# Sharing the centre tap of a row-transformed convolution between even and odd pixels, and squaring two groups of keys in one instruction

## The chip, the cores and the metric

The kernel runs on one core of a Trainium2 chip. The metric is the device time of one execution in microseconds; the time before is the median of three runs. The core has five engines that run beside each other: TensorE (PE in the profile) multiplies matrices and writes to PSUM, VectorE (DVE) and ScalarE (ACT) work element by element and read PSUM or SBUF, GpSimd (POOL) works on SBUF alone, and SyncE (SP) issues nearly all transfers. Everything is fp32.

## The reference

The input has 4 images of 128 channels and 128 x 128 pixels. Layer 0 normalises groups of 4 channels, then treats each pixel as a token of 128 channels:

```
t = LN0(x);  t = t + (silu(LN1(t)) @ W_out.T)
wht = LN2(t) @ W_whiten.T
k = square(relu(wht @ W_key.T))            # 512 hidden keys
t = t + sigmoid(wht @ W_recep.T) * (k @ W_value.T)
```

It does that for the image and for its transpose. No step mixes pixels, so both give the same, and x = x + 2t. Layer 1 normalises groups again and computes

```
x + (conv3x3(gn(x), weight[0], padding 1) + bias) * sigmoid(relu(avg @ w1.T) @ w2.T)
```

The weights of the convolution are always expert 0's, 128 to 128 channels.

## The kernel before, in words

**Layer 0** works on groups of 1024 pixels (`layer0(g)`, g from 0 to 63, 16 for each image), each of two halves of 512 (h = 0, 1). A half's tokens are normalised three times (`norm`, statistics by `bn_stats` on DVE at L770, roots by POOL at L820), go through attention (`att`, L954) and are turned back to channels by way of a DRAM buffer. Then the half has four blocks of 128 keys (j = 0 to 3): a matmul `pk` (L1033) into PSUM, `re` on ACT (L1038: relu and bias, PSUM to an SBUF tile `h`), a square, and a matmul `kv` (L1071) that adds the block's values in one PSUM bank. The squares are on ACT in place (`sq`, L1044), or on DVE as (key + bias) times the rectified key (`sqd`, L1050). `SQUARES` gives the engine for each block: DDAA for both halves while g is under 17, AAAA after.

**Layer 1** works on blocks of 16 rows (`conv(k)`, k from 0 to 31, 8 for each image). The block has four sets of four rows, and a transform along the rows makes six products from six shifted rows: DVE forms v0 to v5 from the rows by sums and differences (L1179 to L1193, twelve instructions of 512 elements, both inputs in SBUF), TensorE convolves each along the row with its own three transformed taps (`product(i)`, three matmuls at L1203 to L1205), and the results m0 to m5 are combined to four output rows: ACT moves m1 and m3 to SBUF (`e`, L1218 and L1226), DVE does the rest (`ab`, `cd`, `y`, L1222 to L1239). The columns shifted by one pixel leave out the edge, hence 512, 508 and 508 columns. `conv_setup(b)` scales the taps (`us`, L621) and adds the identity to four centre taps (`ut2`, L627), once for each image.

**The order.** Each instruction is entered in a planner (`op`, class `Plan`) with its engine, an estimated cost, a priority (its group number plus `SHIFT` by name), what it reads and writes, and the buffers it opens. The planner plays the whole program through once with these costs and fixes the order on each engine; each engine then runs its instructions in that order. `LOOK` and `HASTE` weigh priority against readiness, `ROOM` gives the number of buffers of each kind (PSUM: `Bh` 3 for keys, `Bkv` 1, `Btr` 2 for attention and transposes, `Bconv` 2 for products), and `port` marks instructions that the planner keeps apart on DVE and POOL. The convolution of image b has priorities that lie among the groups of image b + 1, so it runs beside layer 0 of the next image; the last image's convolution has nothing beside it.

**The start.** All of image 0 is loaded in eight pieces and its statistics are taken on DVE; their aggregate (L493) goes to PE as small matmuls (L498, L500) for the group means. `FIRST_FILL` puts warm-up matmuls (`hot`, L411) on PE when the pieces 6 and 7 arrive, three and two of them; more are put into planned gaps of PE early on (`busy`).

Of the kernel before, what the change touches and what calls it, by code (L numbers as in the profile page):

```python
# [23 lines left out]
    "R": -94.694, "Rc": 15.085, "Rm": -2.646, "S": 24.009, "T": -84.8, "Tz": -36.19, "W": -22.14,  # L24
    "ab": 37.315, "att": 1.644, "b": 31.731, "bn0": 11.794, "bn1": -17.35, "bn2": -15.592,
    "bx": 49.609, "c": 7.82, "cag": 6.719, "cav": -18.068, "cd": -103.804, "cp": -37.768,
    "cp1": -27.368, "cpm": -17.233, "cpr": -71.755, "cpv": -65.194, "cre": 48.407, "crt": -73.005,
    "csg": -26.086, "csp": -39.311, "cth": -29.247, "cve": 53.942, "e": 12.136, "e0": 14.7,
    "e1": -70.81, "e2": -55.971, "edge": 60.492, "fw": 14.887, "g": -16.106, "gag": -13.379,
    "gnb": -14.148, "gpm": -2.701, "gpv": -23.531, "grt": -1.635, "gsp": -6.989, "gve": -30.013,  # L30
    "hot": -13.329, "in": 26.361, "in0": 105.375, "kv": 3.816, "late": 12.753, "m0": 23.5,
    "m1": -101.213, "o": -54.585, "pk": 3.497, "pq": -18.954, "pr": 3.288, "q": -106.007,
    "raw": -61.508, "rc": -6.337, "re": -93.796, "silu": -97.676, "sq": -115.033, "sqd": -34.912,
    "t": -2.49, "tD": -49.255, "tR": 16.588, "tW": -20.948, "th": -60.823, "tt": 105.266,
    "u": 16.271, "us": -19.465, "ut": 67.807, "ut2": 9.337, "uw": -50.513, "v": 57.985, "w": 117.982,
    "w0": 44.736, "w1": -43.048, "w2": -6.943, "x": 70.181, "x1": -70.076, "xc": 6.78, "xd": 2.407,
    "xf": -58.371, "xo": -10.863, "xs": -54.606, "y": 24.867, "z": 15.121, "zD": 21.243,
    "zR": 18.813, "zW": -13.966,
}
SQUARES = (("DDAA", "DDAA"), ("AAAA", "AAAA"))  # L40
TAIL_BANKS = ("Bkv", "Btr", "Btr", "Bh", "Bconv", "Bh")
TAIL_HOMES = ("xc", "xc", "x", "x", "x", "xc", "xc", "x")
CONV_AT, CONV_STEP = 2.0, 2.0
LOOK = {'PE': 0.018, 'DVE': 0.087, 'ACT': 0.048, 'POOL': 0.004, 'SP': 0.048}
HASTE = 31.975
SQUARES_AT = 17
ROOM = dict(
    x=3, xd=2, xs=2, ut=3, t=7, z=2, y=2, zd=2, zc=2, td=2, tt=2, R=2, y2=2, h=6, r=2, xc=2, vt=3, v=4,
# [3 lines left out]
BACKLOG = 1.96  # L52
FIRST_U_ON_DVE = (2, 3)


XF_BUS, FIRST_XD, LATE_AT = 3.4, -25, -5
FILL_UNTIL, FILL_STEP = 330, 1.2
FIRST_FILL = {6: 3, 7: 2}
# [26 lines left out]
def S_ON(g):  # L85
    return "POOL" if T_BY_DMA(g) else "DVE"

# [155 lines left out]
def conv_preact_kernel(  # L243
# [42 lines left out]
        z=[P, SUB, C], y=[P, CH], y2=[P, CH], h=[P, CH], r=[P, CH],  # L286
        xc=[P, BLK_ROWS + 2, W], vt=[P, Q, W], v=[P, Q, W], yt=[P, Q, W], uw=[P, 3, P],
# [17 lines left out]
    def staged(name, n, src=None):  # L305
        t = sb.tile([P, n], F32, tag="h", name=name, bufs=ROOM["h"])
        if src is not None:
            nc.scalar.dma_start(t, src)
        return t
# [112 lines left out]
    READ, WRITE = (0, 0.85), (0, 0.4)  # L422

    def op(name, eng, cost, prio, emit, reads=(), writes=(), new=(), port=False, bus=0.0):
        return plan.op(name, eng, cost, prio + SHIFT.get(name, 0.0), emit, reads, writes, new, port, bus)
# [112 lines left out]
    def conv_setup(b, at):  # L538
# [90 lines left out]
        for i in (1, 2, 3, 4, 0, 5):  # L629
            t = ("uw", b, i)  # L630
            if b > 0:

                def fetch(i=i, t=t):
                    nc.sync.dma_start(make(t, "uw"), raw_u[i])

                op("uw", D, READ, at - 1, fetch, [(("raw", i), 0), (("ready", b - 1), 0)], [(t, 0)], [(t, "uw")], bus=0.65)
            op(
                "us", V, (0.52, 0.61), at, lambda i=i: scaled(i), [(c, 0), (t, 0)],
                [(t, 0), *([(("ready", b), 0)] if i == 5 else ())], (), True,
            )  # L640
            if i in TAP:
                op("ut2", V, (0.21, 0.29), at, lambda i=i: tapped(i), [(t, 0)], [(t, 0)], (), True)

# [92 lines left out]
    def layer0(g):  # L736
# [3 lines left out]
        if p * PAIR % PER == 0:  # L740
# [6 lines left out]
            for q in range(SUB):  # L747

                on_dve = k == 0 and q in FIRST_U_ON_DVE

                def lay(q=q, on_dve=on_dve):
                    rs, nb = gn0[b]
                    scale, bias = rs[:, q : q + 1], nb[:, q : q + 1]
                    if on_dve:
                        nc.vector.tensor_scalar(T[xd][:, q], T[xd][:, q], scale, bias, ALU.mult, ALU.add)
                    else:
                        nc.scalar.activation(T[xd][:, q], T[xd][:, q], AF.Identity, bias=bias, scale=scale)

                op(
                    "u", V if on_dve else A, (0.61, 0.7) if on_dve else (0.705, 0.82), g, lay, [(("gn0", b), 0), *((xd, a) for a in range(SUB))],  # L760
                    [(xd, ("u", q))],
                )
# [117 lines left out]
        for h in range(PAIR):  # L880
            r = (p * PAIR + h) % PER

            def turn(h=h, r=r):
# [5 lines left out]
                "ut", V, (0.61, 0.7), g, turn, [(xd, ("u", q)) for q in range(SUB)],  # L889
# [105 lines left out]
        for h in range(PAIR):  # L995
# [33 lines left out]
            for j in range(NH):  # L1029
                pk, hh = ("pk", g, h, j), ("h", g, h, j)  # L1030
# [6 lines left out]
                def relu(pk=pk, hh=hh, j=j):  # L1037
                    nc.scalar.activation(make(hh, "h"), T[pk], AF.Relu, bias=kbias[:, j : j + 1])  # L1038

                op("re", A, (0.572, 0.69), g, relu, [(pk, 0)], [(hh, 0)], [(hh, "h")])  # L1040
                if square_on(g, h, j) == "A":

                    def square(hh=hh):
                        nc.scalar.activation(T[hh], T[hh], AF.Square)  # L1044

                    op("sq", A, (0.52, 0.63), g, square, [(hh, 0)], [(hh, 0)])
                else:

                    def square(pk=pk, hh=hh, j=j):
                        nc.vector.scalar_tensor_tensor(  # L1050
                            T[hh], T[pk], kbias[:, j : j + 1], T[hh], ALU.add, ALU.mult
                        )

                    op("sqd", V, (0.605, 0.685), g, square, [(hh, 0), (pk, 0)], [(hh, 0)])
# [11 lines left out]
            for j in range(NH):  # L1066

                def value(j=j, kv=kv, h=h):
                    if j == 0:
                        make(kv, "Bkv")  # L1070
                    nc.tensor.matmul(T[kv], wv[:, j, :], T["h", g, h, j], start=(j == 0), stop=(j == NH - 1))  # L1071
# [3 lines left out]
                    [(("wv", "c"), 0), (("h", g, h, j), 0), *([(kv, j - 1)] if j else ())],  # L1075
# [32 lines left out]
    def conv(k, at):  # L1108
# [29 lines left out]

        def units(s):
# [8 lines left out]
        def put(n, tag):  # L1148
            if tag == "v" and ending:
                t = sb.tile([P, CH], F32, tag="h", name=n, bufs=ROOM["h"])  # L1150
                T[name_of(n)] = t.rearrange("p (q w) -> p q w", w=W)
                return T[name_of(n)]
            return make(name_of(n), tag)

        def do(name, eng, cost, fn, reads=(), writes=(), new=(), port=False):
            new = [(t, "h" if tag == "v" and ending else tag) for t, tag in new]
# [3 lines left out]
        TWO = (0.605, 0.685)  # L1160

        def inner(name, tag, fn, rows_in=(), tiles_in=(), extra=(), cost=TWO, inplace=False):
# [7 lines left out]
            else:  # L1170
                reads += [(("turned", k - 1, half), v) for v in HALVES[half]]
            do(
                "v" if tag == "v" else "pq", V, cost, fn, reads + ([(t, 0)] if inplace else []), writes,
                () if inplace else [(t, tag)], True,
# [3 lines left out]

        inner("p", "vt", lambda: stt(put("p", "vt"), rows(2), -4.0, rows(4), ALU.mult, ALU.add), (2, 4))  # L1179
        inner("q", "vt", lambda: stt(put("q", "vt"), rows(1), -4.0, rows(3), ALU.mult, ALU.add), (1, 3))  # L1180
        inner(
            "v1", "v", lambda: stt(put("v1", "v"), get("p"), gn["mg6"], get("q"), ALU.add, ALU.add), (),  # L1182
            ("p", "q"), [(("gn1", b), 0)], (0.655, 0.73),
        )
        inner("v2", "v", lambda: tt(put("v2", "v"), get("p"), get("q"), ALU.subtract), (), ("p", "q"))
        inner("p2", "vt", lambda: tt(put("p2", "vt"), rows(4), rows(2), ALU.subtract), (2, 4))
        inner("q2", "vt", lambda: tt(put("q2", "vt"), rows(3), rows(1), ALU.subtract), (1, 3))
        inner("v3", "v", lambda: stt(put("v3", "v"), get("q2"), 2.0, get("p2"), ALU.mult, ALU.add), (), ("p2", "q2"))
        inner("v4", "v", lambda: stt(put("v4", "v"), get("q2"), -2.0, get("p2"), ALU.mult, ALU.add), (), ("p2", "q2"))
        inner("v0a", "v", lambda: tt(put("v0", "v"), rows(0), rows(2), ALU.subtract), (0, 2))  # L1190
        inner("v0b", "v", lambda: stt(get("v0"), get("v0"), 4.0, get("p2"), ALU.mult, ALU.add), (), ("p2",), inplace=True)
        inner("v5a", "v", lambda: tt(put("v5", "v"), rows(5), rows(3), ALU.subtract), (5, 3))
        inner("v5b", "v", lambda: stt(get("v5"), get("q2"), -4.0, get("v5"), ALU.mult, ALU.add), (), ("q2",), inplace=True)  # L1193

        def product(i):
            tag = TAIL_BANKS[i] if ending else "Bconv"
            m, v = name_of(f"m{i}"), name_of(f"v{i}")

# [9 lines left out]

        def t0(n):
            return (name_of(n), 0)  # L1210

        def outer(name, fn, reads, writes, new=(), port=False):
# [5 lines left out]
            lambda: nc.scalar.activation(put("e1", "yt"), get("m1"), AF.Identity, bias=gn["beta"]),  # L1218
            [t0("m1"), (("gn1", b), 0)], [t0("e1")], [(name_of("e1"), "yt")],
        )  # L1220
        product(2)
# [4 lines left out]
            "e", A, (0.572, 0.69), lambda: nc.scalar.copy(put("e3", "yt"), get("m3")), [t0("m3")],  # L1226
            [t0("e3")], [(name_of("e3"), "yt")],
        )
        product(4)
# [91 lines left out]
```

## Time and profile before

| | us |
|---|---|
| median of 3 runs | 1742.97 (1740.23 to 1747.48) |
| profiled execution | 1742.63 |
| its span, first to last instruction | 1740.9 |
| busy: PE, DVE, ACT, POOL | 1690.7, 1424.9, 1293.8, 1184.0 |
| granted TensorE clock | 0.997 |

Busy time is that in which at least one instruction of the engine was in flight. In the groups, a row gives the line of the kernel, the engine, the operation, output and inputs with shapes and the count, then the busy time, the mean time of one in ns, and the idle time of the engine before them with what ended it. An fp32 matmul shows as two records, and instructions in sequence overlap a little: for what one costs in a row, the timeline's starts are compared.

### The profile page before, as it was taken

The numbers are of one execution on the slowest core, as the hardware profiler recorded it, in microseconds if no ns is written. First come the engines' busy times: TensorE is split into PE (matmuls) and PEld (weight loads), VectorE is DVE, ScalarE is ACT, GpSimd is POOL, SyncE is SP. The second block draws the span as 40 slices with busy tenths as digits, with TensorE's granted clock in tenths as the row PEclk, the third lists the DMA queues.
The fourth block names the chain that finished last, engine by engine and source line by source line (L and its number), as shares of the span: only waits on it lengthen the run. The fifth ranks groups of instructions, "written<-read, shape, count | busy, mean of one in ns | idle before, by whom it ended". The sixth has DMA issues, their size and how long they took to land.

```text
span 1740.9 us, 18709 instructions
## 1 busy us (share of the span) xinstructions
PE 1690.7 (97%) x4872; PEld 815.7 (47%) x4872; DVE 1424.9 (82%) x2619; ACT 1293.8 (74%) x2656; POOL 1184.0 (68%) x1085
## 2 busy tenths in 40 slices
PE   5899999999999999999999999999999999999999
PEld 2444544444444445444445445454544444444443
DVE  5898888788889967798998887888897766448986
ACT  1999998898988887889889877998887875440000
POOL 1778887788987885879777886988878773310000
PEclk9999999999999999999999999999999999999999
DMA  9366675466577777578778877577776565215321
GB/s 326 91 213 202 193 219 194 145 206 230 153 250 246 252 230 236 199 232 247 250 245 245 254 238 240 178 218 236 241 254 199 183 204 176 101 75 224 154 98 73
DMA packets 140170, 354.66 MB, mean 204 GB/s; under 512 B 19079, under 2 KB 78750, under 8 KB 122782
## 3 DMA queue, kind: packets, MB, share of 16 engines
q1 hardware_dynamic: 139472, 352.99, 63.1%
q8 instruction: 39, 0.64, 0.2%
q14 instruction: 69, 0.57, 0.1%
q10 hardware_dynamic: 590, 0.46, 0.1%
HBM read 230.31 MB, written 123.07 MB: 203 GB/s over the span
## 4 chain that ended last, share of the span: by engine, by line
PE 71%; ACT 10%; POOL 8%; DVE 7%; DMA 2%; issue 2%; SPq 0%; ACTq 0%; DVEq 0%; POOLq 0%
PE kv L1071 19%; PE pk L1033 18%; PE m L1203 7%; PE m L1204 7%; PE m L1205 7%; PE att L954 5%; PE pr L1058 5%; ACT t L839 2%; ACT h L1038 2%; POOL rs L820 2%; ACT z L839 2%; DVE st L770 1%; ACT h L1044 1%; POOL x L1026 1%; POOL t L908 1%
## 5 line engine op out<-in xcount | busy, mean ns | idle before, releaser
L1071 PE MATMUL kv<-h,wv 128*128 128x512 f32 x1024 | 525.8, 598 | 4.6 <-DVE r L1080 2.6
L1033 PE MATMUL pk<-y,wk_s 128*128 128x512 f32 x1024 | 480.9, 595 | 4.7 <-ACT h L1038 3.1
L1038 ACT ACTIVATE h<-pk,kbias 128x512 f32<-128x512 f32 x512 | 336.1, 682 | 90.9 <-PE pk L1033 88.3
L1033 PEld LDWEIGHTS pk<-y,wk_s 128*128 128x128 f32 x1024 | 190.0, 190 | 239.3 <-issue 178.1
L1071 PEld LDWEIGHTS kv<-h,wv 128*128 128x128 f32 x1024 | 183.0, 190 | 205.3 <-issue 164.1
L1044 ACT ACTIVATE h<-h 128x512 f32<-128x512 f32 x444 | 267.5, 629 | 2.6
L1086 POOL TENSOR_TENSOR x<-x,r 128x512 f32<-128x512 f32 x128 | 169.8, 1327 | 132.0 <-DVE r L1080 128.5
L820 POOL TENSOR_TENSOR rs<-rs,nhalf 128x8 f32<-128x8 f32 (+1 forms) x134 | 227.2, 1700 | 47.3 <-ACT rs L817 45.1
L839 ACT ACTIVATE z<-t,nb,rs 128x128 f32<-128x128 f32 x512 | 208.7, 489 | 21.8 <-POOL nb L825 20.9
L839 ACT ACTIVATE t<-ut,nb,rs 128x128 f32<-128x128 f32 x512 | 209.7, 488 | 8.5 <-POOL nb L825 4.8
L908 POOL TENSOR_TENSOR t<-t,g 128x512 f32<-128x512 f32 x124 | 161.2, 1301 | 68.0 <-ACT t L839 67.6
L770 DVE BATCH_NORM_STATS2 st<-t 128x6 f32<-128x256 f32 x512 | 187.1, 410 | 22.9 <-POOL t L911 22.7
L1203 PE MATMUL m<-v,uw 128*128 128x512 f32 x384 | 197.7, 596 | 3.9 <-DVE v L1182 3.9
L1204 PE MATMUL m<-v,uw 128*128 128x508 f32 x384 | 195.4, 590 | 0.0
L1205 PE MATMUL m<-v,uw 128*128 128x508 f32 x384 | 194.9, 589 | 0.0
L1015 POOL TENSOR_TENSOR y<-tt,R 128x512 f32<-128x512 f32 x96 | 130.9, 1367 | 59.8 <-PE pk L1033 46.9
L1026 POOL TENSOR_TENSOR x<-tt,x 128x512 f32<-128x512 f32 x124 | 162.5, 1324 | 3.9 <-DMA tt<-ts 3.7
L911 POOL TENSOR_TENSOR t<-t,b 128x512 f32<-128x512 f32 x124 | 162.7, 1319 | 2.6
L954 PEld LDWEIGHTS att<-wo,y 128*128 128x128 f32 x1024 | 130.9, 192 | 51.7 <-issue 33.1
L1063 ACT ACTIVATE r<-pr,rbias 128x512 f32<-128x512 f32 x128 | 87.1, 681 | 72.6 <-PE pr L1058 36.2
L1058 PE MATMUL pr<-y,wr_s 128*128 128x512 f32 x256 | 132.3, 600 | 3.9 <-ACT h L1038 3.0
L954 PE MATMUL att<-wo,y 128*128 128x128 f32 x1024 | 132.8, 276 | 0.4 <-ACT y L947 0.3
(160 smaller groups left out, 2278.6 us busy)
## 6 DMA issues: line engine op xcount, KB each, us to landing
xd<-in_x SPq DMA_DIRECT2D x128, 256.0 KB
x<-in_x SPq DMA_DIRECT2D x32, 1024.0 KB
xo<-x SPq DMA_DIRECT2D x32, 1024.0 KB
R<-rd SPq DMA_DIRECT2D x63, 512.0 KB
ts<-td SPq DMA_DIRECT2D x248, 128.0 KB
tt<-ts SPq DMA_DIRECT2D x62, 512.0 KB
out<-xc SPq DMA_DIRECT2D x31, 1024.0 KB
xc<-xo SPq DMA_DIRECT2D x24, 1152.0 KB
```

The lines of the kernel that those rows point to most:

```text
L770: nc.vector.bn_stats(st[:, i : i + 2, :].rearrange("p n f -> p (n f)"), two)
L820: nc.gpsimd.tensor_tensor(T[rs][:, part], T[rs][:, part], nhalf[:, :k], ALU.pow)
L839: nc.scalar.activation(dst[:, s, :], src[:, s, :], AF.Identity, bias=nb[:, i : i + 1], scale=rs[:, i : i + 1])
L954: nc.tensor.matmul(pa[:, ts(m, P)], T[y][:, ts(m, P)], wo2, start=True, stop=True)
L1033: nc.tensor.matmul(make(pk, "Bh"), wk_s[:, ts(j, P)], T[y2], start=True, stop=True)
L1038: nc.scalar.activation(make(hh, "h"), T[pk], AF.Relu, bias=kbias[:, j : j + 1])
L1044: nc.scalar.activation(T[hh], T[hh], AF.Square)
L1058: nc.tensor.matmul(make(pr, "Bh"), wr_s, T[y2], start=True, stop=True)
L1071: nc.tensor.matmul(T[kv], wv[:, j, :], T["h", g, h, j], start=(j == 0), stop=(j == NH - 1))
L1203: nc.tensor.matmul(pc, u[:, 1], vv, start=True, stop=False)
L1204: nc.tensor.matmul(pc[:, :, 1:W], u[:, 0], vv[:, :, 0 : W - 1], start=False, stop=False)
L1205: nc.tensor.matmul(pc[:, :, 0 : W - 1], u[:, 2], vv[:, :, 1:W], start=False, stop=True)
```

## The change

Write x[2k] and x[2k+1] for even and odd pixels, and u0, u1, u2 for a product's three taps. Then

```
y[2k]   = u1 (x[2k] + x[2k+1]) + (u2 - u1) x[2k+1] + u0 x[2k-1]
y[2k+1] = u1 (x[2k] + x[2k+1]) + (u0 - u1) x[2k]   + u2 x[2k+2]
```

The first term is shared. In the products 0, 1, 3 and 5 of images 0 to 2 (`PARITY`), v is stored as an even half and an odd half (elements 256 positions apart), DVE adds the halves (`su`, 256 elements), PE computes the shared term once in the first half of a `Btr` bank (`cm`) and the four other terms in half-size matmuls (`c`), and DVE adds the shared term to both pixels after the result has been moved or summed (`cs`, reading PSUM). The differences of taps are made once for each image and product (`ud`). Products 2 and 4, and all of image 3, stay as they were.

The tile `h` now holds two blocks of keys, three tiles in place of six. A `W` in `SQUARES` squares both blocks in one ACT instruction of 1024 elements; for g under 17 three squares of a group are on DVE in place of four, one is a single on ACT and four are two wide ones.

The rest: one buffer in place of two for `zd` and `td`, the last image's v and some set-up tiles in another buffer, new values in `SHIFT`, `LOOK` and `HASTE`, three warm-up matmuls fewer. What `FIRST_U` adds leaves the engines of the first block's four instructions as they were; `RUSH`, `SUMS_ON_POOL` and the squares on POOL (`P`) are empty.

```diff
-SQUARES = (("DDAA", "DDAA"), ("AAAA", "AAAA"))
+SQUARES = (("DAWW", "DDWW"), ("WWWW", "WWWW"))
+SUM_BANK = "Btr"
-LOOK = {'PE': 0.018, 'DVE': 0.087, 'ACT': 0.048, 'POOL': 0.004, 'SP': 0.048}
-HASTE = 31.975
+LOOK = {'PE': 0, 'DVE': 0, 'ACT': 0.177, 'POOL': 0, 'SP': 0.026}
+HASTE = 75.103
 ROOM = dict(
-    x=3, xd=2, xs=2, ut=3, t=7, z=2, y=2, zd=2, zc=2, td=2, tt=2, R=2, y2=2, h=6, r=2, xc=2, vt=3, v=4,
+    s=2, ud=4,
+    x=3, xd=2, xs=2, ut=3, t=7, z=2, y=2, zd=1, zc=2, td=1, tt=2, R=2, y2=2, h=3, r=2, xc=2, vt=3, v=4,
...
-XF_BUS, FIRST_XD, LATE_AT = 3.4, -25, -5
+XF_BUS, FIRST_XD, LATE_AT = 3.2, -25, -5
-FIRST_FILL = {6: 3, 7: 2}
+FIRST_FILL = {7: 2}
...
+def PARITY(k):
+    return (0, 1, 3, 5) if k < 24 else ()
...
+                    nc.vector.tensor_tensor(make(ud, "ud"), u[:, 0::2], u[:, 1:2].to_broadcast([P, 2, P]), ALU.subtract)
+                op("ud", V, (0.335, 0.42), at, beside, [(t, 0)], [(ud, 0)], [(ud, "ud")], True)
...
+                elif how == "W" and not first:
                     def square(hh=hh):
-                        nc.scalar.activation(T[hh], T[hh], AF.Square)
+                        x = T[hh].rearrange("p a b -> p (a b)")
+                        nc.scalar.activation(x, x, AF.Square)
+                    op("sq", A, WIDE, g, square, [(hh, 0), (hh, 1)], [(hh, 0), (hh, 1)])
...
+            if tag == "v" and int(n[1]) in halves:
+                whole = T[name_of(n)].rearrange("p q w -> p (q w)")
+                T[name_of(n)] = whole.rearrange("p (e q k) -> p q k e", e=2, q=Q)
...
+                    nc.vector.tensor_tensor(dst, x[:, 0], x[:, 1], ALU.add)
+                do("su", V, (0.335, 0.42), both, [(v, 0)], [(su, 0)], [(su, "s")], True)
...
+                    bank = make(m, tag)
+                    pc = bank.rearrange("p (e q k) -> p e q k", e=2, q=Q)
+                    T[m] = bank.rearrange("p (e q k) -> p q k e", e=2, q=Q)
+                    u, d, x = T["uw", b, i], T[ud], flat_halves(i)
+                    nc.tensor.matmul(pc[:, 0], d[:, 1], x[:, 1], start=True, stop=False)
+                    nc.tensor.matmul(pc[:, 0, :, 1:], u[:, 0], x[:, 1, :, : W // 2 - 1], start=False, stop=True)
+                    nc.tensor.matmul(pc[:, 1], d[:, 0], x[:, 0], start=True, stop=False)
+                    nc.tensor.matmul(pc[:, 1, :, : W // 2 - 1], u[:, 2], x[:, 0, :, 1:], start=False, stop=True)
+
+                def shared():
+                    nc.tensor.matmul(make(mm, SUM_BANK)[:, : CH // 2], T["uw", b, i][:, 1], T[su], start=True, stop=True)
...
+            def add():
+                t = by_parity(get(n))
+                row = T[name_of(f"mm{i}")][:, : CH // 2].rearrange("p (q k o) -> p q k o", q=Q, o=1)
+                tt(t, row.to_broadcast([P, Q, W // 2, 2]), t, ALU.add)
+            do("cs", V, TWO, add, [(name_of(f"mm{i}"), 0), t0(n)], [t0(n)])
...
         product(0)
-        outer("y", lambda: tt(rows(1), get("m0"), get("c"), ALU.add), [t0("m0"), t0("c")], units(1))
+        with_shared(0, "c")
+        outer("y", lambda: tt(par(0, rows(1)), get("m0"), par(0, get("c")), ALU.add), [t0("m0"), t0("c")], units(1))
```

## The prediction

> **What bounds the kernel now.** I read the page first: TensorE is busy in nine tenths or more of nearly every slice.
>
> ```profile
> PE 1690.7 (97%) x4872; PEld 815.7 (47%) x4872; DVE 1424.9 (82%) x2619; ACT 1293.8 (74%) x2656; POOL 1184.0 (68%) x1085
> ...
> PE   5899999999999999999999999999999999999999
> ...
> DVE  5898888788889967798998887888897766448986
> ```
>
> The average hides three stages, so I cut the span where the first convolution products begin (about 425) and where the last image's convolution is left alone (about 1575). The view by stretches gives busy microseconds for each engine:
>
> ```profile
> 0.00:425.00 425.00, 386.19 (x1273) 197.55 (x1274) 351.15 (x689) 359.93 (x766) 316.98 (x329) 0.99 0.65 203
> 425.00:1575.00 1150.00, 1146.34 (x3228) 548.18 (x3227) 934.30 (x1692) 920.94 (x1869) 865.23 (x755) 1.00 0.67 212
> 1575.00:1741.00 166.00, 158.12 (x373) 69.98 (x371) 139.49 (x240) 12.98 (x22) 1.83 (x2) 0.99 0.37 144
> ```
>
> In order: PE, weight loads, DVE, ACT, POOL, clock, DMA share, GB/s. The middle stage, where 88 of the 96 changed products run, has PE busy 1146.3 of 1150, the granted clock at 1.00: PE alone sets its length. DVE is busy 934 of 1150, 81%. The waits say the same from the other side: PE hardly waits for the convolution's inputs, while DVE waits for PE (columns: us in total, times, longest; the second line is from 425 to 1400).
>
> ```profile
> PE m L1203 <- DVE v L1182: 3.9, 2, 3.4
> ...
> DVE r L1080 <- PE kv L1071: 28.2, 24, 4.5
> ```
>
> **The change, part by part.**
>
> **TensorE, the four products.** Before, a product is three fp32 matmuls of 512, 508 and 508 columns, each two records; after, five of 256, 252, 256, 252 and 256. PE's timeline shows what records cost from start to start:
>
> ```profile
> 819.84 1.02 PE L1203 MATMUL m<-v,uw 128*128 128x512 f32 x2
> ...
> 822.40 1.02 PE L1071 MATMUL kv<-h,wv 128*128 128x512 f32 x2
> ...
> 825.82 1.95 PE L954 MATMUL att<-wo,y 128*128 128x128 f32 x16
> 827.61 1.02 PE L1071 MATMUL kv<-h,wv 128*128 128x512 f32 x2
> ```
>
> A product takes 822.40 - 819.84 = 2.56 us. A 512-column record takes 0.430 (0.86 for two), a 128-column one (827.61 - 825.82) / 16 = 0.112. Between them the slope is 0.828 ns a column, so 256 columns take 0.218 and 252 take 0.215. The new product: 6 x 0.218 + 4 x 0.215 = 2.17 us, 0.39 less. Four products of eight blocks of three images are 96: **-37.9 us** on the engine that sets the end. The shorter records do not expose their weight loads: L954 loads weights before every 128-column record and still starts one each 0.112 us.
>
> **VectorE, added.** For each product one sum of the halves (su, 256 elements, both inputs in SBUF) and one add of the shared half into the result (cs, 512 elements, one input in PSUM). The trace has neither; nearest are these groups from 425 to 1575 (busy, mean ns, idle before):
>
> ```profile
> L770 DVE BATCH_NORM_STATS2 st<-t 128x6 f32<-128x256 f32 x348 | 127.0, 410 | 17.8 <-POOL t L911 17.6
> L1094 DVE BATCH_NORM_STATS2 st<-x 128x6 f32<-128x512 f32 x93 | 63.1, 679 | 24.1 <-POOL x L1086 23.7
> ...
> L1189 DVE SCALAR_TENSOR_TENSOR v<-q,p 128x512 f32<-128x512 f32 x22 | 23.3, 1058 | 4.7 <-PE m L1205 4.7
> ...
> L1237 DVE TENSOR_TENSOR xc<-m,c 128x512 f32<-128x512 f32 x22 | 14.9, 679 | 2.8 <-PE m L1205 2.6
> ```
>
> cs is like L1237, 0.68, of which 0.07 overlaps the next one (back-to-back 512-element instructions start 0.61 apart): 0.61. su at 256 elements is 0.41. But instructions with two SBUF inputs also stand still while POOL works: L1189 shows 1058 against 679, and the sixteen such groups of a block average 849, 0.17 over. I give su 0.50 (between 0.35 and 0.58). For 88 products 88 x 1.11 = 98, and eight weight differences (ud) in the stage at about 0.41, some 4: **+102 us of DVE**. DVE then needs 934 + 102 = 1036 us in a stage that PE would finish in 1150 - 88 x 0.39 = 1115: **93%**. None of it is on the critical path so long as DVE keeps up. Can it? In single stretches it did, PE full beside it (PE, weight loads, DVE, ...):
>
> ```profile
> 925.00:950.00 25.00, 25.00 (x84) 13.09 (x83) 24.54 (x53) 24.55 (x50) 17.79 (x15) 1.00 0.83 245
> ```
>
> A mean of 93% leaves 79 us of gaps where there were 216, in an order fixed beforehand. When a DVE instruction is late, its product is late on PE, and the key matmuls of the other image queued behind it on PE too. Cs waits for the shared matmul; queued behind it on DVE are statistics and transposes which feed ACT and DMA. I take **+7 us** of new PE waits (0 if DVE's slack always covers; 30 if it mostly doesn't).
>
> **Where a rule of the skill speaks against it.** v1, v3, v0 (two instructions) and v5 (two) now write even and odd elements 1 KB apart, and four results are read from PSUM in that order. The Trainium skill, "SBUF — State Buffer" (section "Door 1: The DMA port swizzle"), says that SBUF has 16-byte lines and each access to a new line pays, so fp32 steps are free only up to 4 elements; PSUM's lines are given as 8 bytes. Here every access changes line. Row L770 tests it for reads: it alternates between positions 512 bytes apart, and takes 410 for 256 elements. L1094 reads 512, in rows of 128 that lie together, and takes 679: the 256 elements more cost 269, 1.05 ns each. At twice that price L770's elements alone would take 538, more than its whole 410. So alternating reads pay no line penalty, and I go by the row: 0. By the rule, if a new line doubles an element's time (my estimate for "pays"), 0.53 us x 8 DVE instructions x 22 blocks is 93 us more DVE, 1129 in all, more than PE's 1115, and the sum is 1781 (below). Strided writes and PSUM reads have no row, so this end stays open.
>
> **ScalarE, wide squares.** From image 1 on, eight squares become four of 1024 elements.
>
> ```profile
> L1044 ACT ACTIVATE h<-h 128x512 f32<-128x512 f32 x368 | 220.4, 628 | 2.3
> ...
> L839 ACT ACTIVATE z<-t,nb,rs 128x128 f32<-128x128 f32 x352 | 143.2, 488 | 21.7 <-POOL nb L825 20.9 <-DVE zd L850 0.8
> ...
> L757 ACT ACTIVATE xd<-xd,nb,rs 128x512 f32<-128x512 f32 x80 | 61.4, 808 | 0.0
> ```
>
> L839 to L757 is 320 ns for 384 elements, 0.833 each. A wide square is 628 + 427 = 1055, occupying about 0.95 against 2 x 0.52: 0.09 saved, 188 pairs, 17 us of ACT. ACT is at 80% in the middle stage: no time. The first value matmul of a pair waits for the second key; PE's other image covers that. If it didn't: 1 us a pair.
>
> **The first stage** (image 0 alone, 17 groups of 1024 positions). DVE squares fall from 4 to 3 a group (-10 us of DVE); ACT goes from four single squares (2.08) to one and two wide (0.52 + 1.90 = 2.42): +0.34, 5.8 us in 17 groups. From 100 to 425 ACT is busy 297 of 325, and PE idles 10.7. I take **+2** (-2 to +5.8).
>
> **The start.** The warm-up matmuls on the seventh load go (three of five). They are on the chain: the means wait behind them on PE.
>
> ```profile
> 31.04 1.02 DVE L493 BATCH_NORM_AGGREGATE mv<-st 128x2 f32<-128x192 f32 x1
> ...
> 29.49 7.20 PE L411 MATMUL fill<-xf,gmat 128*128 128x512 f32 x10
> 36.53 0.95 PE L498 MATMUL pm<-mv,gturn 128*128 128x1 f32 x8
> ```
>
> The aggregate is done at 32.06, its matmul starts at 36.53. Four records in place of ten, 0.704 each, end at 32.3: **-4** (0 if a cooler clock takes it back).
>
> **At nothing:** one buffer in place of two for the transposed tiles (td, zd): a group uses each once in about 25 us and its stores take under 10; if DMA is late, DVE stands behind them. The keys' memory is the same (six tiles, three doubles). The shared products take one of two PSUM banks of attention (Btr) until cs has read them; if PE had to wait for that, up to 0.7 us a product, 65 us. The new priorities move the order of everything; with PE full, order alone gains little. The tail keeps its products.
>
> **Sum.** The profiled execution took 1742.6 (span 1740.9 and 1.7 around it), 0.4 below the median of the runs, 1742.97. 1742.6 - 37.9 - 4 + 2 + 7 = 1709.7: **1710**.
>
> **Rivals.** (1) **DVE becomes the bound in part.** If waits in its fixed order hold it to 91 or 92% of the middle stage, that takes 1036 / 0.915 = 1132, 17 over PE: in all 1742.6 - 18 - 4 + 2 = 1723; at 90% (1151) the stage gains nothing and the result is 1742. For it: 81% now, stretched two-input instructions. Against: slices at 98%, and the slack after 1400, where DVE is busy 103 of 175, into which late blocks can move. (2) **Slower: strided writes and PSUM reads pay.** 1129 us of DVE at 95% is 1188, 38 over 1150, beginning at 1742.6 + 38: 1781. It decides from 0.32 us an instruction (0.95 x 1150 = 1093, less 1036, over 176). Against it L770; for it that nothing writes so yet. (3) **No saving arrives**, because shared products hold attention's banks: 0.4 us a product suffices, 1743. Against: DVE reads a product's result soon, L1237 idles little.
>
> **Chances.** Nearly the full saving, 1696 to 1718: 0.62. DVE-limited gain, 1718 to 1734: 0.25. Cancelled, 1734 to 1752: 0.06. Slower: 0.07. 0.5% (8.7 us) is about what a measurement of this kernel can tell from no change. So faster 0.87, same 0.06, slower 0.07. The low end: all bounds good, 1742.6 - 37.9 - 4.2 - 2 = 1698.5, and 2 us of idle start: 1696. The high end takes in the DVE-limited case: 1733.
>
> **What would show it.** Ten records a product, 2.17 us from start to start; su near 0.41 to 0.58, cs near 0.68; v groups no longer than now; DVE about 93% and PE 99% of a middle stage of some 1120; means at 32 to 33. Wrong if PE shows waits for v, su or cs that sum over 20 us, if strided groups exceed their old means by 0.3 us, or if attention waits for banks.

## The result

The changed kernel takes 1746.3 us (median of 20 runs, 1741.4 to 1755.5) beside 1743.7 for the kernel before (20 runs, 1740.2 to 1748.3): a ratio of **1.0014, interval 1.0004 to 1.0024**. Nothing was gained (if anything, some 2.5 us were lost), where 1710 was forecast, in a range of 1696 to 1733. The profiled execution has a span of 1744.0 us, against 1740.9, at a granted clock of 0.996.

The page after, the line of busy times and two lines of the 40 slices:

```profile
PE 1659.6 (95%) x5250; PEld 879.9 (50%) x5250; DVE 1556.7 (89%) x2806; ACT 1285.9 (74%) x2451; POOL 1212.7 (70%) x1085
...
PE   5899999998999999999999999999999999997999
...
DVE  6898877889999999999999999899989897758896
```

PE has 31 us less to do than before and the span is 3 us longer. DVE has 132 us more; from the tenth slice to the thirty-third it now shows a 9 in all but three. The same three stretches as before (columns: PE, weight loads, DVE, ACT, POOL, clock, DMA share, GB/s):

```profile
0.00:425.00 425.00, 386.75 (x1294) 197.83 (x1294) 354.63 (x703) 374.02 (x769) 327.41 (x341) 1.00 0.67 208
425.00:1575.00 1150.00, 1117.48 (x3564) 607.59 (x3565) 1060.21 (x1863) 896.47 (x1658) 882.16 (x742) 1.00 0.67 213
1575.00:1744.00 169.00, 155.32 (x394) 74.52 (x392) 141.86 (x241) 15.40 (x25) 3.09 (x3) 0.97 0.33 128
```

In the middle stretch PE is idle for 32.5 us where it was for 3.7, although the clock is still 1.00, and DVE is at 1060 of 1150, 92%. What PE waits for from 425 to 1600 (us in total, times, longest), and below it the largest entry of the same view before:

```profile
PE mm L1302 <- DVE s L1281: 13.1, 14, 2.1
PE m L1296 <- DVE v L1253: 4.4, 4, 1.9
...
PE mm L1302 <- DVE e L1325: 1.6, 1, 1.6
PE kv L1116 <- DVE r L1125: 1.6, 4, 0.5
PE att L979 <- DVE t L984: 1.3, 2, 1.2
```

```profile
PE pk L1033 <- ACT h L1038: 1.3, 4, 0.8
```

L1302 is the shared product, which waits for its sum of halves, or until a shared addition has emptied its bank; L1296 is a product that waits for v; L1116 is layer 0's value matmul and L979 attention, which wait until DVE has emptied their banks. All of these stand behind DVE. One more long wait lies behind the stretch: a single stall at 1605, before the first product of the last image.

```profile
PE m L1312 <- DVE v L1253: 8.7, 1, 8.7
```

The groups of DVE from 425 to 1575:

```profile
L1281 DVE TENSOR_TENSOR s<-v 128x256 f32<-128x256 f32 x91 | 59.0, 648 | 0.1
...
L1251 DVE TENSOR_TENSOR v<-xc 128x512 f32<-128x512 f32 x45 | 52.4, 1168 | 6.5 <-PE m L1299 6.5
L1325 DVE TENSOR_TENSOR e<-mm,e 128x512 f32<-128x512 f32 x67 | 45.0, 671 | 0.0
...
L1253 DVE SCALAR_TENSOR_TENSOR v<-v,p 128x512 f32<-128x512 f32 x23 | 29.3, 1274 | 0.2
...
L1251 DVE TENSOR_TENSOR v<-p,q 128x512 f32<-128x512 f32 x22 | 15.5, 706 | 0.0
L1363 DVE TENSOR_TENSOR xc<-m,c 128x512 f32<-128x512 f32 x22 | 15.0, 681 | 0.2
```

The last but one, `v<-p,q`, is v2, which is still written in line: 706 ns. The others shown that write v write even and odd elements 1 KB apart: 1168 and 1274. In these means are instructions that were held up for long, as before the change (the prediction shows one group at 1058). The medians are little moved by those. Least, median and longest ns, after the change, then before it:

```profile
L1251 DVE TENSOR_TENSOR v<-xc x45: 1028/1072/2155, 447.6 to 1558.5; 128x512 f32<-128x512 f32 x45
L1251 DVE TENSOR_TENSOR v<-p,q x22: 640/682/1300, 465.3 to 1533.8; 128x512 f32<-128x512 f32 x22
...
L1253 DVE SCALAR_TENSOR_TENSOR v<-v,p x23: 1044/1089/1922, 440.4 to 1555.5; 128x512 f32<-128x512 f32 x23
```

```profile
L1191 DVE SCALAR_TENSOR_TENSOR v<-v,p x32: 647/684/1806, 435.4 to 1714.7; 128x512 f32<-128x512 f32 x32
...
L1190 DVE TENSOR_TENSOR v<-xc x32: 672/685/1154, 433.6 to 1714.0; 128x512 f32<-128x512 f32 x32
```

**Each strided write costs 0.39 us more** (1072 against 685; 0.40 for `v<-v,p`). There are six in a block (v1, v3, two for v0, two for v5), 144 in all: 56 us. The additions themselves, `e<-mm,e` at 671, and the results read from PSUM in that order, L1363 at 681, cost what an ordinary instruction costs.

To place the loss in time I compared each PE record's distance to the next one with its own cost (0.828 ns a column and 5.9 ns, the line through the two spacings in the prediction). The own costs sum to 1645.7 before and 1604.7 after: **41.0 us less**. Of these, 38.4 are the products, the saving that was promised, and 2.6 the three warm-up matmuls that went. The rest, in which PE is late or idle, grew from 84.6 to 127.8: 3.6 less in the first 100 us, 4.7 less up to 400, **43.8 more from 400 to 1600**, 7.8 more at the end. Of the 7.8, 5.3 are the stall before the last image's first product (8.9 against 3.6 on this scale); the rest goes with the granted clock, which was 0.50 to 0.52 from 1610 to 1620, where before it was 0.68 from 1610 to 1615 and 0.98 after that.

### The profile page after: what moved, and what is told of

It reads as the page before. It is cut to its first block, busy times and chain, and to the rows that moved or that the text cites. A ratio compares the mean times of both kernels' runs of the same rounds, so it can differ in the third digit from the quotient of the medians.

```text
span 1744.0 us, 19588 instructions
## 1 busy us (share of the span) xinstructions
PE 1659.6 (95%) x5250; PEld 879.9 (50%) x5250; DVE 1556.7 (89%) x2806; ACT 1285.9 (74%) x2451; POOL 1212.7 (70%) x1085
## 4 chain that ended last, share of the span: by engine, by line
PE 39%; DVE 26%; POOL 14%; ACT 11%; DMA 6%; issue 4%; SPq 1%; ACTq 0%; DVEq 0%; POOLq 0%
PE kv L1116 9%; PE pk L1058 9%; DVE st L795 4%; PE m L1312 3%; PE m L1314 3%; PE m L1313 3%; POOL rs L845 3%; ACT t L864 3%; PE pr L1103 3%; PE att L979 2%; ACT h L1064 2%; DVE v L1253 2%; ACT z L864 2%; POOL y L1040 2%; POOL x L1051 2%
## 5 line engine op out<-in xcount | busy, mean ns | idle before, releaser
L1116 PE MATMUL kv<-h,wv 128*128 128x512 f32 x1024 | 521.2, 595 | 10.4 <-DVE r L1125 8.7
L1058 PE MATMUL pk<-y,wk_s 128*128 128x512 f32 x1024 | 496.2, 597 | 5.8 <-ACT h L1064 2.9
L1064 ACT ACTIVATE h<-pk,kbias 128x512 f32<-128x512 f32 x512 | 341.3, 681 | 108.9 <-PE pk L1058 81.8
L1116 PEld LDWEIGHTS kv<-h,wv 128*128 128x128 f32 x1024 | 187.6, 190 | 182.5 <-issue 142.1
L1083 ACT ACTIVATE h<-h 128x1024 f32<-128x1024 f32 x222 | 234.1, 1054 | 1.9
L933 POOL TENSOR_TENSOR t<-t,g 128x512 f32<-128x512 f32 x124 | 165.6, 1338 | 73.6 <-ACT t L864 67.0
L936 POOL TENSOR_TENSOR t<-t,b 128x512 f32<-128x512 f32 x124 | 169.8, 1375 | 3.4
L979 PEld LDWEIGHTS att<-wo,y 128*128 128x128 f32 x1024 | 128.7, 191 | 53.9 <-issue 28.1
L979 PE MATMUL att<-wo,y 128*128 128x128 f32 x1024 | 133.4, 277 | 4.3 <-ACT y L972 1.6
L816 POOL TENSOR_TENSOR four<-four,nhalf 128x8 f32<-128x8 f32 x63 | 109.6, 1742 | 22.3 <-ACT four L812 19.5
L1312 PE MATMUL m<-v,uw 128*128 128x512 f32 x192 | 99.8, 601 | 10.9 <-DVE v L1253 8.7
L1125 DVE SCALAR_TENSOR_TENSOR r<-r,kv 128x512 f32<-128x512 f32 x128 | 86.4, 675 | 26.5 <-PE kv L1116 25.3
```

Source lines behind the costliest of these rows:

```text
L936: eng.tensor_tensor(T[t], T[t], over(b0), ALU.add)
L979: nc.tensor.matmul(pa[:, ts(m, P)], T[y][:, ts(m, P)], wo2, start=True, stop=True)
L1058: nc.tensor.matmul(make(pk, "Bh"), wk_s[:, ts(j, P)], T[y2], start=True, stop=True)
L1064: nc.scalar.activation(dst[:, j % 2], T[pk], AF.Relu, bias=kbias[:, j : j + 1])
L1083: nc.scalar.activation(x, x, AF.Square)
L1116: nc.tensor.matmul(T[kv], wv[:, j, :], T["h", g, h, j // 2][:, j % 2], start=(j == 0), stop=(j == NH - 1))
```

## The experiments

The theory after the result: the strided writes make DVE so full that v, the sums and the emptied banks come late, and PE's waits eat the saving (S). Rivals: the sums and the shared additions do it, whatever the writes cost (C); the new order of the instructions does it (O); attention's PSUM banks, which the shared products borrow, do it (B).

**v written in line.** v keeps its old layout; TensorE and the sums read every second element instead. The order and every cost in the planner stay as in the changed kernel.

```diff
-            if tag == "v" and int(n[1]) in halves:
-                whole = T[name_of(n)].rearrange("p q w -> p (q w)")
-                T[name_of(n)] = whole.rearrange("p (e q k) -> p q k e", e=2, q=Q)
...
-            return by_parity if int(n[1]) in halves else (lambda ap: ap)
+            return lambda ap: ap
...
-            return T[name_of(f"v{i}")].rearrange("p q k e -> p e q k")
+            return T[name_of(f"v{i}")].rearrange("p q (k e) -> p e q k", e=2)
```

> The changed kernel, except that v0, v1, v3 and v5 are written in line, as before, and PE and su read even and odd elements with a step of two. The order on every engine is the same. Theory S (the writes 1 KB apart cost 0.39 us each, 144 of them 56 us, and tip DVE over): the strided v instructions fall from a median of 1.05 to 1.14 us to about 0.69, DVE needs some 50 us less in the middle stage, PE stops waiting for su and v, time 1705 to 1718. Rival D (su, cs and the waits for POOL fill DVE even so): half of that at most, 1730 to 1740. Rival O (the new order or the shared PSUM banks are what delays PE): 1741 to 1748. If PE reads slowly with a step of two, its records of 256 columns exceed 0.215 us from start to start and the time rises.

Measured: **1724.5 us** (1722.3 to 1727.7), ratio 0.9891 (0.9867 to 0.9914). It is faster than both kernels, by this edit alone, but it lies between the ranges: S had asked for 1718 at most, rival D of the expectation for 1730 at least. Its middle stretch:

```profile
425.00:1575.00 1150.00, 1139.51 (x3637) 623.66 (x3637) 1024.09 (x1898) 899.43 (x1665) 861.84 (x747) 1.00 0.67 215
```

Its waits over the whole span (all 6.0 of L1116 fall in the first 425 us) and two of DVE's groups:

```profile
PE m L1309 <- DVE v L1250: 8.7, 1, 8.7
PE kv L1116 <- DVE r L1125: 6.0, 6, 2.9
...
PE mm L1299 <- DVE s L1278: 3.1, 4, 2.0
```

```profile
L1278 DVE TENSOR_TENSOR s<-v 128x256 f32<-128x256 f32 x94 | 53.4, 568 | 0.1
...
L1248 DVE TENSOR_TENSOR v<-xc 128x512 f32<-128x512 f32 x47 | 37.2, 793 | 7.8 <-PE m L1296 7.8
```

DVE is 57 us less busy over the whole span (1499.6 against 1556.7), about the 56 us of the writes; PE's wait for the sums falls from 13.1 to 3.1, and PE's lateness from 400 us to just before the last image's first product falls from 43.8 us over before to 21.5 over it. Something of these 21.5 is the price of the edit. PE's timeline for four half-size matmuls, first of the changed kernel, then of this one, from the first to what follows the fourth:

```profile
1430.90 0.59 PE L1296 MATMUL m<-v,ud 128*128 128x256 f32 x2
...
1432.61 1.02 PE L1116 MATMUL kv<-h,wv 128*128 128x512 f32 x2
```

```profile
1557.92 0.61 PE L1293 MATMUL m<-v,ud 128*128 128x256 f32 x2
...
1559.73 0.59 PE L1116 MATMUL kv<-h,wv 128*128 128x512 f32 x1
```

1.71 us with halves that lie together, 1.81 with every second element: 0.10 us a product, some 10 us for 96. So it costs TensorE 10 us to read the pixels of one parity from a row, and it cost DVE 56 to lay them apart.

**Without the shared addition.** The changed kernel with the instruction `cs` left out, so that the centre tap's shared term is missing from the output of four products; writes, sums and order stay.

```diff
-                tt(t, row.to_broadcast([P, Q, W // 2, 2]), t, ALU.add)
+                del t, row
```

> The changed kernel without the instructions that add the shared term (cs), so the four products lack their centre tap; everything else in the same order, the strided writes included. DVE has 96 x 0.61 = 59 us less to do, about what the strided writes cost. S and D (DVE is the bound) both expect 1705 to 1720; O expects no gain, 1741 to 1748.

Measured: 1730.4 us (1728.8 to 1734.5), ratio 0.9926 (0.9902 to 0.9951), 10 us above the expected range. DVE's busy time falls to 1030.9 in the middle stretch and by 44 us over the span (1512.3), less than the 59 that were reckoned. Relief taken from a wholly different instruction, with every strided write in place, brings back 15.9 us, where 57 us of relief had brought 21.8 together with TensorE's dearer reads. So DVE's load counts, and not the strided write alone. Two things blur the comparison: without the addition nothing reads the shared product, so its bank is free at once (PE's waits for such banks came to 3.4 us, see below), and v in line is also ready 0.39 us sooner at each write.

**Both together.** v in line, and no shared addition.

```diff
 (the kernel with v in line)
-                tt(t, row.to_broadcast([P, Q, W // 2, 2]), t, ALU.add)
+                del t, row
```

> v in line, and the shared add left out (the products lack their centre tap), all in the changed kernel's order. If DVE still sets part of the time with v in line, taking 59 us from it brings 8 to 15 us more: 1709 to 1717. If what is left of the loss is PE's reads with a step of two (0.0225 us more for each of 384 matmuls, 8.6 us) and the end's stall (PE 8.7 us without work before the last image's products), it stays within 1720 to 1726.

Measured: 1720.6 us (1719.0 to 1722.0), ratio 0.9868 (0.9844 to 0.9892), in the second of the expected ranges, which put what is left down to TensorE's reads and the stall at the end. The middle stretch:

```profile
425.00:1575.00 1150.00, 1141.18 (x3654) 625.97 (x3653) 989.04 (x1807) 900.24 (x1668) 869.88 (x748) 1.00 0.67 215
```

The four kernels share one order and form a square:

| middle stretch, DVE busy / time | with the shared addition | without it |
|---|---|---|
| v apart | 1060 / 1746.3 | 1031 / 1730.4 |
| v in line | 1024 / 1724.5 | 989 / 1720.6 |

The shared addition costs 15.9 us in the first row and 3.9 in the second. The same relief is worth four times as much where the writes are strided: there is a load beyond which DVE sets the time, in this order somewhere near 90% of the stretch (1024 to 1060 us are 89 to 92%). Load alone does not explain all four: by my estimate TensorE's strided reads take 10 us of each in-line kernel (0.10 x 96). Without them v in line would stand at some 1715, and 7 us more load (1031 against 1024) would go with some 16 us more time (1730). How much of that is v being ready later, these runs don't separate. Theory C falls as far as the shared additions go: with v in line they are nearly free. The sums are in all four kernels. The square also leaves a floor. With DVE at 86%, 1720.6 is still 10 us over the forecast, about what TensorE's strided reads cost.

**The probe.** A kernel of its own that computes nothing of the reference: instructions of 512 elements in a row, with results and inputs in different places, to price the write by itself.

```
put("d_line", CH, lambda t: tt(t, a, b, ALU.add))
put("d_apart", CH, lambda t: tt(parted(t), by(a), by(b), ALU.add))
put("d_apart_stt", CH, lambda t: stt(parted(t), by(a), 2.0, by(b), ALU.mult, ALU.add))
put("d_step2", 2 * CH, lambda t: tt(t.rearrange("p (n s) -> p n s", s=2)[:, :, 0], a, b, ALU.add))
...
put("d_from_apart", CH, lambda t: tt(by(t), parted(a), parted(b), ALU.add))
...
put("s_apart", CH, lambda t: nc.scalar.copy(parted(t), by(a)))
...
```

> Not the task's computation: a row of single instructions, six of each kind, with POOL idle while DVE works. S: adding 512 elements takes 0.68 us when they are written in line and 1.05 to 1.07 when even and odd ones go 1 KB apart; reading from such places costs nothing (0.68). A model with a price for each new 16-byte line would show 0.68 for a write step of 2 elements and the high price from a step of 4 on. PE: 256 columns start 0.215 to 0.22 us apart from every source. ScalarE and GpSimd writes: open.

`parted` lays even and odd elements 1 KB apart; the cuts (...) hold the steps of 4 and 8, a read with a step of 8, the other copies, and the same on GpSimd and TensorE. The groups of DVE and ACT (L48 writes in line, L49 apart, as does L50; L51, L52 and L53 write with steps of 2, 4 and 8 elements; L58 reads with a step of 8; L55 reads what lies apart):

```profile
L49 DVE TENSOR_TENSOR d_apart<-a,b 128x512 f32<-128x512 f32 x6 | 12.9, 2145 | 0.0
...
L48 DVE TENSOR_TENSOR d_line<-a,b 128x512 f32<-128x512 f32 x6 | 9.3, 1550 | 0.1
...
L58 DVE TENSOR_TENSOR d_from_step<-two,a 128x512 f32<-128x512 f32 x6 | 6.8, 1129 | 0.0
L61 ACT COPY s_apart<-a 128x512 f32<-128x512 f32 x6 | 6.7, 1124 | 0.0
L53 DVE TENSOR_TENSOR d_step<-a,b 128x512 f32<-128x512 f32 x6 | 6.3, 1058 | 0.0
L52 DVE TENSOR_TENSOR d_step<-a,b 128x512 f32<-128x512 f32 x6 | 6.3, 1044 | 0.0
...
L51 DVE TENSOR_TENSOR d_step<-a,b 128x512 f32<-128x512 f32 x6 | 4.1, 676 | 0.0
L55 DVE TENSOR_TENSOR d_from_apart<-a,b 128x512 f32<-128x512 f32 x6 | 4.0, 672 | 0.0
L60 ACT COPY s_line<-a 128x512 f32<-128x512 f32 x6 | 3.8, 635 | 1.5 <-DMA a<-in_x 1.5
```

And for L50 the least, median and longest, as its first one still met POOL:

```profile
L50 DVE SCALAR_TENSOR_TENSOR d_apart_stt<-a,b x6: 1030/1036/2071, 24.9 to 33.3; 128x512 f32<-128x512 f32 x6
```

L48 and L49 ran while POOL was at work on the same inputs, against the expectation, and give no price by themselves: 1550 and 2145. The in-line write to compare with is the kernel's, 682 to 685. Writing with a step of 2 (8 bytes) is free, 676. A step of 4 (16 bytes) costs 1044, and 8 no more, 1058; a step of 3 was not run. Laying results 1 KB apart has a median of 1036 on DVE (L50). So the price is some 0.37 us for 512 elements, where it is paid. Reading shows why the prediction was misled: a read with a step of 8 pays too, 1129, but a read that alternates between two places 1 KB apart does not, 672. ACT pays more for writing apart (1124 against 635). On TensorE a record of 256 columns starts 216 ns after the last when its input lies together, 227 with a step of 2, as in the kernel, and 431 with a step of 16, where the expectation had 215 to 220 from every source.

**The cost told to the planner.** The changed kernel again, with 0.385 us added to the planner's figure of 0.605 for a strided write, and one priority changed.

```diff
+            if tag == "v" and int(name[1]) in halves:
+                cost = (cost[0] + 0.385, cost[1] + 0.385)
...
-    "uw": -45.697, ...
+    "uw": -150, ...
```

> The changed kernel, v written apart as there, but the planner is told what these writes cost (0.385 us more for each of the 144), and the taps' loads (uw) get a higher priority without which it finds no order. The order changes everywhere. S: DVE has the same work as in the changed kernel, so knowing its price brings little: 1728 to 1745. O (a wrong order alone is the fault): 1705 to 1718, as with v in line or better.

Measured: 1735.7 us (1730.9 to 1741.8), ratio 0.9961 (0.9947 to 0.9974). The same instructions as in the changed kernel, 10.6 us less, within the range of S. The order had been laid out as if a strided write cost what another does.

**v apart, with all priorities made anew.** A step further: 0.42 for a sum as well, and the priorities chosen so that the planner's own end is least.

```diff
+            if tag == "v" and int(name[1]) in halves:
+                cost = (cost[0] + 0.385, cost[1] + 0.385)
...
-                do("su", V, (0.335, 0.42), both, [(v, 0)], [(su, 0)], [(su, "s")], True)
+                do("su", V, (0.42, 0.5), both, [(v, 0)], [(su, 0)], [(su, "s")], True)
...
-CONV_AT, CONV_STEP = 2.0, 2.0
+CONV_AT, CONV_STEP = 1.654, 2.074
...
-HASTE = 75.103
+HASTE = 21.056
```

(and new numbers in `SHIFT`)

> The changed kernel with every instruction it has, v still written apart, but with the order fitted to measured costs: the planner is told 0.385 us more for each strided write of v and 0.42 for a sum of halves, and the priorities are chosen anew until the planner's own end is least (1685.9 with these costs; the earlier kernels' spans came 31 to 38 us above a plan with true costs). Theory A (the strided writes cost DVE 56 us, and the loss comes from DVE being late in an order that was made for cheap writes): an order made for the true costs hides part of it, 1717 to 1726. Theory B (DVE at 92% is simply too full, in any order): within 5 of the earlier kernel with planned costs, 1730 to 1740.

Measured: 1731.4 us (1725.3 to 1732.6), ratio 0.9922 (0.9903 to 0.994). In its middle stretch:

```profile
425.00:1575.00 1150.00, 1129.85 (x3612) 618.97 (x3613) 1071.60 (x1890) 900.38 (x1658) 861.43 (x736) 1.00 0.67 213
```

DVE is busier than in the changed kernel, 1071.6 us, 93%, and PE is idle 20 us where it was 32.5. It lies 5 us or more above what the first theory of its expectation asked for, and within the second's. Both hold in part: with costs nearer the measured ones another order takes back 15 of the 22 us that the writes cost in the first, so 93% is not a wall, and the point at which DVE sets the time is a property of the order.

**v in line, with all priorities made anew.** The in-line kernel with 0.09 us more for the four half-size matmuls, 0.42 for a sum, and `SHIFT`, `HASTE`, `CONV_AT` and `CONV_STEP` chosen in the same way.

```diff
-                do("su", V, (0.335, 0.42), both, ...
+                do("su", V, (0.42, 0.5), both, ...
-                do("c", E, (1.72, 1.79), parts, ...
+                do("c", E, (1.81, 1.88), parts, ...
```

> v written in line, TensorE and the sums reading every other element, and the order fitted in the same way to measured costs (0.09 us more for the four half-size matmuls of a product, 0.42 for a sum of halves); the planner's end is 1678.7, against 1690.1 for the in-line kernel's old priorities with these costs. If that kernel's remaining loss (1724.5, with 8.7 us before the last image's first product and 6 us for gated sums) is one of order: 1709 to 1716. If it is contention that the planner doesn't see: 1721 to 1727, no better than the in-line kernel before.

Measured: 1731.1 us (1726.1 to 1735.5), ratio 0.9929 (0.991 to 0.9947): 7 us **slower** than the in-line kernel with the old order, where the plan had promised 11 us less. Both expectations were missed. Its waits:

```profile
PE mm L1300 <- DVE s L1279: 9.0, 8, 2.5
...
PE m L1310 <- DVE uw L641: 5.7, 1, 5.7
```

The stall before the last image's first product is shorter and now waits for the scaled taps (L1310, 5.7 us, where it waited 8.7 for v), and the sums of halves are late again, 9.0 us against 3.1. An order worth 11 us in the plan cost 7 on the chip, so differences of some 10 us in the plan say little.

With the orders made anew, v apart and v in line take the same time, 1731.4 and 1731.1. The 22 us between them are thus shown for one order only; in another order the strided writes need not cost the kernel anything, and as orders alone move the time by 7 to 15 us, no price of the layout can be read from the second pair.

**Products 1 and 3 alone.** `PARITY` gives (1, 3); the planner lays out a new order for it.

```diff
-    return (0, 1, 3, 5) if k < 24 else ()
+    return (1, 3) if k < 24 else ()
```

> The changed kernel with the shared tap in products 1 and 3 only. PE saves 48 x 0.42 = 20 us; DVE gets 48 strided writes (19 us) and 48 su and cs (55 us) in place of 144 (56) and 96 (110). S and D: DVE stays under its limit, so the halved change brings nearly all of its 20 us and the start's 4: 1718 to 1728, faster than both kernels. O: the loss is not DVE's, the gain is eaten as with four products, 1738 to 1748.

Measured: 1773.0 us (1769.6 to 1778.4), ratio 1.0161 (1.0134 to 1.0188). It was expected to gain (1718 to 1728 by S, 1738 to 1748 by O) and is the slowest of all, outside both, with PE idle for 43 us of the middle stretch and DVE at 983, 85%. Its waits:

```profile
PE kv L1116 <- DVE r L1125: 11.6, 13, 2.1
PE m L1312 <- DVE v L1253: 8.2, 1, 8.2
PE pk L1058 <- POOL y L1040: 7.1, 5, 3.5
...
PE m L1312 <- DVE uw L640: 4.6, 1, 4.6
```

PE waits for banks, v, POOL and taps, in an order that the priorities had not been chosen for; the granted clock of the run was 0.987, and PE's lateness 142 us. This does not price the strided writes, but it counts against S as the whole story: at 85% DVE was not too full, and PE waited more than in the changed kernel. An edit which changes the plan can lose some 30 us by the order; the square above, whose kernels keep one order, is what the cause rests on.

**No shared products at all.** `PARITY` gives nothing: wide squares, new priorities and the shorter warm-up stay.

```diff
-    return (0, 1, 3, 5) if k < 24 else ()
+    return ()
```

> The changed kernel with all six products whole again; wide squares, new priorities, buffers and start stay. PE has its 41 us back, DVE loses su, cs and the strided writes. S: what is left of the change is worth about the start's 4 us: 1735 to 1745. O: the new order costs time also without the sharing: 1755 to 1785.

Measured: 1747.6 us (1743.5 to 1750.5, 20 runs), ratio 1.0021 (1.0012 to 1.003). One of its waits:

```profile
PE m L1312 <- DVE v L1253: 7.1, 2, 6.8
```

It lies above the 1735 to 1745 of S and far below the 1755 of O. The rest of the change, in the order that it then has, is worth nothing, rather 4 us less than nothing. The stall before the last image's first product, 6.8 us here and 8.7 in the changed kernel (3.4 before), is there without any shared product: it comes with the rest of the change (priorities, buffers and the wide squares, which no run separates). PE's lateness from 400 to 1600 is 6.7 us over before here, with DVE at 914 us of the stretch.

**The shorter warm-up alone,** in the kernel before.

```diff
-FIRST_FILL = {6: 3, 7: 2}
+FIRST_FILL = {7: 2}
```

> The kernel before with only the change at the start: two warm-up matmuls in place of five, the same order otherwise. The means start at 32.5 in place of 36.5, and the time is 3 to 4.5 us shorter, 1739 to 1741; or, if a cooler TensorE or the next loads take it back, within 1 us of before.

Measured: 1740.9 us (1734.8 to 1743.9, 20 runs), ratio 0.9982 (0.9972 to 0.9993), 3.1 us, as expected. The means' matmuls start at 32.79, not at 36.53.

## Why the prediction was wrong

**The step that failed** stands under "Where a rule of the skill speaks against it": "So alternating reads pay no line penalty, and I go by the row: 0." The row was read rightly. Alternating reads are free, also in the probe (672). But the change writes in that pattern, and a write is another matter: 0.39 us more for each, 56 us for 144. Writing in line again, with the order kept, brought back 21.8 us of the 36.6 between forecast and result. The Trainium skill's page "SBUF — State Buffer" (section "Door 1: The DMA port swizzle") had the rule that counted for the writes, 16-byte lines, a price for each new one, and at least two hits on a line to hide it: step 2 (two hits on each line) is free at 676, step 4 (one hit) is not at 1044. Its limit of 4 fp32, which the prediction repeated, is too far for writes by these runs. A read that alternates does not follow the rule (672), and my row happened to be just that. The end of 0.53 us for eight instructions was too high, 0.39 for six is what it was. The text said that no row showed strided writes and left the end open, and then gave it 7 in 100.

**TensorE's work:** right. -37.9 forecast; a product costs 2.15 us from start to start, not 2.17, which makes some -40 for 96 (-38.4 by the line through the two spacings), and weight loads stayed hidden.

**DVE's added work:** short by the writes, and su was taken too small. DVE went from 934 to 1060 us in the middle stretch, 126 more, where 102 were forecast. cs was as forecast (671 to 678 ns each). su has a median of 0.42 us but a mean of 0.65, beyond the end of 0.58 that I gave; with v in line the mean is 0.57. POOL's hold as its cause I argue from the pairs of median and mean, and from the probe, where an in-line addition took 1550 ns beside POOL; no run took POOL's work away.

**"I take +7 us of new PE waits (0 ...; 30 ...)":** this is where the price came due. 43.8 us between 400 and 1600, beyond its end of 30. With the writes in line it was 21.5, and some 10 of these are TensorE's own reads of every second element. So some 12 are left for the load I had assumed, within the term's range, and the term was wrong for the load there was. That 98% was kept up in single stretches of 25 us was no evidence for 92% over 1150.

**Rival (2)** named the mechanism. At 0.39 us for the some 135 strided writes in the stretch, my formula has DVE at 1036 + 53 = 1089, against 1093 at which it was to decide: a gain of nothing, which is what came. That the sum lands there is partly luck: DVE was at 1060, 92% of the stretch and not 95, and the end lost 7.8 us that it does not hold. Rival (1), DVE the bound in part, gave 1742 for DVE held at 90%, from another cause; the square points to such a bound, near 90% in this order. Rival (3), attention's banks: in the changed kernel PE waits 1.6 us in all for a shared addition to empty a bank for the next shared product, and 1.8 for DVE to empty one for attention, so by the waits the banks have hardly a part in the loss; no run frees them alone.

**The small terms.** The start: -4 forecast, 3.8 us sooner in the trace (32.71, not 36.53), 3.1 alone. The first stage: +2 forecast, 4.7 us of PE's lateness gained between 100 and 400. The wide squares: 1055 ns forecast, 1054 measured, and the kernel that has them without shared products gained nothing. "Order alone gains little" missed the loss: the rest of the change put 7.8 us at the end, most of it the stall before the last image's products. Together with TensorE's 10 us of strided reads this is also why 1724.5, the best of the kernels that compute the whole reference, is not at 1710.

Of the 43.8 us in the middle, some 22 are undone by the in-line layout. The rest of it (some 12 us beyond the strided reads) I can't assign to one cause: an emptier DVE took 3.9 us off the time, 6.7 are there without any shared product, and new orders moved the time in both directions.

## What to carry to other kernels

When a layout is changed to help one engine, price the write of it on the engine that makes it: a store whose elements went alternately to two places 1 KB apart cost more than half as much again (0.39 us on 0.68), and the reader could have taken the stride for 0.10 us a product. A row of the trace counts against a rule only if it does the same thing in the same direction; a read says nothing about a write. And in a kernel with a fixed order, work added to a second engine is free only up to a load that this order sets (here near 90%): test one edit at a time with the order held, because a new order alone moved the time by more than the change did.

## What the runs showed of the hardware

- Writing 512 fp32 elements to SBUF with a step of 2 is free on DVE (676 ns), 4 costs 1044, 8 no more than 4 (1058). Results alternating between two places 1 KB apart cost the same as a step of 4 (1036 on DVE), on ACT 1124 against 635.
- Reading is not like writing: alternating between two places 1 KB apart is free on DVE (672), while a step of 8 costs 1129. On ACT it cost 738 against 635.
- TensorE's moving input with every second element cost 1.81 us for four matmuls of 256 and 252 columns where halves that lie together took 1.71; with a step of 16 a record of 256 columns took 431 ns in place of 216.
- DVE reads results from PSUM in alternating places 1 KB apart at 681 and 667 ns, as fast as in line (679 and 681 before).
